# First recurrence steps with plain fp32 state products, weight conversions on VectorE, and four feed-forwards moved to later steps

## The chip, the cores and the metric

The kernel runs on one core of a Trainium2 chip. The metric is the time of one execution in microseconds, as the device reports it; lower is better. All times below are in microseconds unless they carry another unit. Engines are named as the profile names them: PE is TensorE (PEld its loading of the stationary operand), DVE is VectorE, ACT is ScalarE, POOL is GpSimd, and SP is the engine whose queue issues most transfers.

## The reference

The program is two layers. The first, where the change lies, is a GRU over 64 steps and a feed-forward with a ternary weight matrix, added to the input:

```python
def cell(h, x):
    gi = x @ W_ih + b_ih
    gh = h @ W_hh + b_hh
    i_r, i_z, i_n = jnp.split(gi, 3, axis=-1)
    h_r, h_z, h_n = jnp.split(gh, 3, axis=-1)
    r = jax.nn.sigmoid(i_r + h_r)
    z = jax.nn.sigmoid(i_z + h_z)
    n = jnp.tanh(i_n + r * h_n)
    h_new = (1.0 - z) * n + z * h
    return (h_new, h_new)
...
scale = jnp.mean(jnp.abs(weight))
w_t = jnp.clip(jnp.round(weight / (scale + EPS)), -1.0, 1.0)
w_ste = weight + jax.lax.stop_gradient(w_t * scale - weight)
return jnp.einsum('bsi,oi->bso', x, w_ste) + bias
...
x = x + ffn(gru(cond, x))
```

The batch is 128, the width 512, so a state is 128 x 512, and each gate is a product of a 128 x 512 operand with a 512 x 512 matrix. The second layer is a causal convolution over time, a router that sends each row to 6 of 64 experts, and a shared feed-forward; the change does not touch it.

## The kernel before

**The stages.** The GRU takes up to about 1255 us of the span, the convolution follows until about 1320, then the router, the shared feed-forward and the experts. All is one program; each engine runs its instructions in the order in which a scheduler has laid them out, and waits where an operand or a buffer is not ready.

**Products in three parts.** PE multiplies fp32 as such at one speed, and a rounded form (fp32r) faster. So the kernel splits each operand into a high part and a scaled low part and a mix of both, and forms a product as three fp32r products: high by high and low by low into one bank, mix by mix into a second, put together on DVE when the bank is read (`WHOLE`). A product of a 128 x 512 operand with a matrix is four matmuls, one for each 128 rows (`products`, L310 records each matmul). Step 0 alone uses plain fp32 products with the weights as they came from memory (`raw_i`, `raw_h`).

**Splitting a weight** (`convert`, L331): for each of the four pieces of 128 x 512, DVE masks off the low bits (`masked`, L321), ACT copies the result into the high plane, an engine subtracts it in place from the raw weight (L337: POOL for the three w_ih matrices, DVE for the three w_hh), ACT writes the scaled low plane (L338) and DVE the mix (L339). The cuts are a ring of four buffers (`stm`, later `cuts`). All 24 pieces are split ahead of the loop over steps: the w_ih matrices 0, 2, 1, then w_hh 0, 2 and 1. The input x of a step is split by `split_x` (masked on DVE, `xl` on POOL, `xs` on DVE), the turned state by `split_h` (DVE and ACT: `hcut`, `hh`, `hl`, `hs`).

**A step t** (L529): the state products for gates r, n and z (`state_gate`, c = 0, 2, 1), three groups of four matmuls each, are added to what the input products of this step have left in the banks; `split_x(t + 1)`; the cell on DVE and ACT (`cell_r`, `cell_n`, `cell_z`: h is overwritten); the feed-forward of the step before, two groups with the ternary matrix `sgn` (`ffn(t - 1)`); the input products of step t + 1 for gates n and r; the new h turned by four transposes (`turned_up`, L387) and split; the input products for gate z. That is 20 groups of four matmuls and four transposes. Eight banks of PSUM hold it all: two for each gate, one for the transposes (`pst`), one for the feed-forward (`psf`).

**Feed-forward.** `ffn` evacuates psf with the scale and the residual (L411, on DVE), and two stores on SP write the result, one to `x1c` for the convolution (L413), one to `out` (L417). The residual x of a step is loaded by `load_x` (L258) into one of seven slots, three in `io0` (`xn`) and four in a buffer `q` that held a raw w_hh and then the raw feed-forward weight; POOL adds the bias to it (`add_bias`, L263). `sgn` is made by `ternary` (L419) in step 1: four reductions, a product with ones, four comparisons and four `sgn` operations.

**Queues.** SP issues the loads of the weights and biases in the order of their use, then 32 stores of zeros (`x1c<-tab`, 16 KB), the feed-forward weight, and from then on the stores of each step and two transfers for the convolution (`toeplitz`). POOL issues the loads of x and of its transposed form (`xp`), between its own additions; its instructions run in their order, so a load that waits for a slot holds `xl`.

Of the kernel before, what the change touches and what calls it, by code (L numbers as in the profile page):

```python
# [45 lines left out]
def adaln_ffn_kernel(  # L46
# [32 lines left out]

    xts = dram.tile([T // 2, P, D], F32, name="xts")  # L80

    const = ctx.enter_context(tc.tile_pool(name="const", bufs=1))
# [123 lines left out]
    with (  # L206
# [18 lines left out]
        def planes(pool, name):  # L225
            return [pool.tile([P, KD, D], F32R, name=f"{name}{n}") for n in "hls"]
# [6 lines left out]
        st = stage.enter_context(tc.tile_pool(name="st", bufs=1))  # L233
        stm = stage.enter_context(tc.tile_pool(name="stm", bufs=4))
        raw_i = [st.tile([P, KD, D], F32, name=f"rawi{c}") for c in range(3)]
        late = ExitStack()
        raw_h = [
            st.tile([P, KD, D], F32, name="rawh0"),
            wi.tile([P, KD, D], F32, name="q"),
            late.enter_context(tc.tile_pool(name="late", bufs=1, side="right")).tile(  # L240
                [P, KD, D], F32, name="rawh2"
            ),
        ]
        zrow = stm.tile([P, D], F32, name="cut")

# [6 lines left out]

        more = []

        def load_x(t):
            r = (t - 1) % 7
            xn = io0.tile([P, D], F32, name="xn") if t < 3 or r > 3 else more[0][:, r]
            (nc.sync if t < 3 else nc.gpsimd).dma_start(out=xn, in_=x[:, t, :])  # L258
            xns[t] = xn

        def add_bias(t, after):
            with tc.issue_after(after.ins):
                nc.gpsimd.tensor_add(xns[t], xns[t], fb)  # L263

# [12 lines left out]
        load_halves(raw_i[2], w_ih[:, cols[2]])  # L277
        nc.sync.dma_start(out=h, in_=cond)
        load_halves(raw_i[1], w_ih[:, cols[1]])
        load_rows(raw_h[0], w_hh[:, cols[0]])  # L280
# [7 lines left out]
        repeated(bh[1], b_hh[cols[1]])  # L288
        load_xt(1, nc.sync)
        nc.gpsimd.memset(zrow, 0.0)  # L290
# [39 lines left out]

        def convert(raw, dst, engine, pool, name):  # L331

            for k in range(KD):
                cut = pool.tile([P, D], F32, name=name)
                masked(cut, raw[:, k])
                nc.scalar.copy(dst[0][:, k], cut)
                engine.tensor_sub(raw[:, k], raw[:, k], cut)  # L337
                nc.scalar.activation(dst[1][:, k], raw[:, k], AF.Copy, scale=SPLIT)  # L338
                nc.vector.scalar_tensor_tensor(  # L339
                    dst[2][:, k], cut, -1.0 / SPLIT, raw[:, k], ALU.mult, ALU.add  # L340
                )

        def split_x(t):

            xp = xps.pop(t)
            cut = xpp.tile([P, KD, B], F32, name="xcut", bufs=1)
            parts_of[t] = [xpp.tile([P, KD, B], F32R, name=f"x{n}", bufs=1) for n in "hls"]
            xh, xl, xs = parts_of[t]
            masked(cut, xp)
            nc.scalar.copy(xh, cut)  # L350
            return low_parts(nc.gpsimd, xl, xs, xp, cut)

        gis = {}

        def input_gate(t, c):

            xh, xl, xs = parts_of[t]
            wh, wl, ws = wih[c]
            a, b = banks(c)
            products(a, xh, wh, start=True)  # L360
            products(a, xl, wl, stop=c == 2)
            products(b, xs, ws, start=True, stop=c == 2)
            if c != 2:
                gis[t, c] = a, b
                return
            g = el0.tile([P, D], F32, name="gi")
            nc.vector.scalar_tensor_tensor(g, a, WHOLE, bin_, ALU.mult, ALU.add)
            nc.vector.tensor_add(g, b, g)
            gis[t, c] = g

        def state_gate(t, c, parts):

            hh, hl, hs = parts
            wh, wl, ws = whh[c]
            new = c == 2
            a, b = banks(c) if new else gis.pop((t, c))
            products(a, hh, wh, start=new)
            yield
            products(a, hl, wl, stop=True)
            products(b, hs, ws, start=new, stop=True)  # L380
            yield a, b
# [71 lines left out]
        def cell_n(t, ps, r):  # L453
            a, b = ps
            n = el0.tile([P, D], F32, name="n")
            if t == 0:
                nc.vector.tensor_add(n, b, bhn)
# [20 lines left out]

        load_x(0)

        x0 = xps.pop(0)
# [17 lines left out]
        r = cell_r(0, first[0])  # L499
        n = cell_n(0, first[2], r)  # L500
        cell_z(0, first[1], n)
        add_bias(0, split_x(1))
        for c in (0, 2, 1):
            convert(raw_i[c], wih[c], nc.gpsimd, stm, "cut")
        convert(raw_h[0], whh[0], nc.vector, stm, "cut")
        stage.close()
        load_xt(2)
        load_x(1)
        for c, name in ((2, "wh2"), (1, "wh1")):
            whh[c] = planes(  # L510
                wh0.enter_context(tc.tile_pool(name=name, bufs=1, reuse_waits="tile")), f"whh{c}"
            )
            with tc.tile_pool(name="cuts", bufs=4, reuse_waits="tile") as cuts:
                convert(raw_h[c], whh[c], nc.vector, cuts, "cut")
            if c == 2:
                late.close()
        sgn = wh0.enter_context(tc.tile_pool(name="sgn", bufs=1, reuse_waits="tile")).tile(
            [P, KD, D], F32R, name="sgn"
        )
        input_gate(1, 0)  # L520
        pieces = None
        input_gate(1, 2)
        turned = turned_up(h)
        pieces = split_h(turned)
        input_gate(1, 1)
        wf = wi.tile([P, KD, D], F32, name="q")
        load_rows(wf, wfT)

        for t in range(1, T):  # L529
            if t == 1:  # L530
                load_x(2)
            elif t + 3 < T:
                load_x(t + 3)
            if t + 2 < T:
# [3 lines left out]

            gates = [state_gate(t, c, pieces) for c in (0, 2, 1)]
            next(gates[0])  # L540
# [4 lines left out]
            if t + 1 < T:  # L545
                last_low = split_x(t + 1)
                add_bias(t, last_low)
            r = cell_r(t, ps_r)
            n = cell_n(t, ps_n, r)
            cell_z(t, ps_z, n)  # L550
            if t == 1:
                ternary(wf)
                more.append(wi.tile([P, KD, D], F32, name="q"))
                load_x(3)
                load_x(4)
            if t == T - 2:
                add_bias(T - 1, last_low)
            ffn(t - 1, pieces)
            if t + 1 < T:
                input_gate(t + 1, 2)  # L560
                input_gate(t + 1, 0)
                turned = turned_up(h)
                pieces = split_h(turned)
                input_gate(t + 1, 1)
            if t == T - TAIL:
# [1037 lines left out]
```

## Time and profile before

| what | value |
|---|---|
| median of three runs | 2502.7 (2502.47 to 2504.35) |
| the profiled execution | 2501.87 |
| its span, first to last instruction | 2500.2 |
| mean granted clock of TensorE | 0.994 |
| PE busy | 2455.9 (98%) |
| DVE busy | 1544.0 (62%) |
| ACT, POOL busy | 459.9, 457.6 (18% each) |
| bytes moved | 320.24 MB, 128 GB/s on average |

The profile is of one execution. A row of an order of time gives the start, the duration, the engine, the line in the kernel, the operation, its output and inputs by name with their shape, how many instructions were merged into the row, and in brackets how long the engine stood idle before it and what ended the wait. Matmuls overlap, so the distance between the starts of two groups is what a group costs, and the duration of the row is a little longer. A plain fp32 matmul shows as two records, an fp32r one as one. A row for a stretch of time gives for each engine the busy time in it, then the granted clock of TensorE, the share of the transfer engines that was busy, and GB/s.

### The profile page before, as it was taken

To read this page: it belongs to the slowest core of one execution; us is meant where nothing else is said; L and a number is where in the kernel's file an instruction comes from. 1 tells how busy PE (TensorE), PEld (TensorE's weight loads), DVE (VectorE), ACT (ScalarE), POOL (GpSimd) and SP (SyncE) were. 2 spreads that over 40 slices of the span, in tenths; PEclk is the share of its full clock that TensorE was granted. 3 is DMA by queue.
4 is the path that set the end of the run, shared out by engine and by line. 5 is a ranking of instruction groups with operands and counts; after the bars stand their busy time and mean duration, and the time that the engine had idled before them with its cause. 6 is when DMAs were issued, how large, how long until landed. Compare 5 with 4: busy or idle time off the path is not lost.

```text
span 2500.2 us, 32119 instructions
## 1 busy us (share of the span) xinstructions
PE 2455.9 (98%) x12333; PEld 1893.1 (76%) x12333; DVE 1544.0 (62%) x3058; ACT 459.9 (18%) x840; POOL 457.6 (18%) x476
## 2 busy tenths in 40 slices
PE   6899999999999999999989999999999999999999
PEld 3788888888888888888888668888776666666667
DVE  7777777767767777777667556666564333443344
ACT  5111111111111111111112322222221111111111
POOL 4221121121112112112221000000011222222220
PEclk8999999999999999999999999999999999999999
DMA  5433333333322222222388312222368999999962
GB/s 177 87 68 63 64 65 62 61 69 61 59 58 60 51 59 59 51 60 48 76 292 302 95 22 41 55 55 61 91 175 271 289 298 303 284 323 289 288 181 51
DMA packets 463754, 320.24 MB, mean 128 GB/s; under 512 B 316465, under 2 KB 384049, under 8 KB 461425
## 3 DMA queue, kind: packets, MB, share of 16 engines
q1 hardware_dynamic: 435264, 246.08, 34.4%
q0 software_dynamic: 28336, 72.11, 12.8%
q8 instruction: 97, 1.59, 0.3%
q14 instruction: 57, 0.46, 0.1%
HBM read 232.39 MB, written 90.98 MB: 129 GB/s over the span
## 4 chain that ended last, share of the span: by engine, by line
PE 94%; DVE 1%; DMA 1%; issue 0%; SPq 0%; ACT 0%; POOL 0%; DVEq 0%; ACTq 0%
PE psa L310 9%; PE psx L310 9%; PE psw L310 9%; PE psw L762 7%; PE psx L762 7%; PE psz L762 7%; PE psf L310 5%; PE psy L310 5%; PE psz L310 5%; PE psb L310 4%; PE y L762 4%; PE py L1488 3%; PE pg L1462 3%; PE pu L1462 3%; PE y L939 2%; PE psc L188 2%
## 5 line engine op out<-in xcount | busy, mean ns | idle before, releaser
L328 DVE SCALAR_TENSOR_TENSOR xs<-xl,xcut 128x512 fp32r<-128x512 f32 x63 | 109.9, 1744 | 84.7 <-POOL xl L327 84.7
L1472 DVE SCALAR_TENSOR_TENSOR a<-a,rw,pu 128x352 f32<-128x352 f32 x32 | 18.6, 581 | 213.0 <-PE pu L1462 213.0
L321 DVE TENSOR_SCALAR hcut<-pst 128x512 int32<-128x512 int32 x64 | 44.3, 692 | 147.2 <-PE pst L387 147.2
L395 ACT CAST hh<-hcut 128x512 fp32r<-128x512 f32 x64 | 39.8, 621 | 401.6 <-DVE hcut L321 390.6
L1044 POOL DMA_DIRECT2D out_dram<-hid x32 | 27.8, 1026 | 450.6 <-issue 333.7
L327 POOL TENSOR_TENSOR xl<-xp,xcut 128x512 fp32r<-128x512 f32 x63 | 87.2, 1384 | 123.4 <-PE psa L310 99.4
L450 ACT ACTIVATE rz<-rz 128x512 f32<-128x512 f32 x64 | 40.5, 633 | 351.1 <-DVE rz L449 349.3
L258 POOL DMA_DIRECT2D q<-in_x_dram x34 | 18.3, 538 | 450.0 <-DVE hcut L321 157.8
L1488 PE MATMUL py<-wd,aeT 128*64 128x512 f32 (+1 forms) x384 | 88.8, 597 | 0.0
L258 POOL DMA_DIRECT2D xn<-in_x_dram x27 | 14.5, 538 | 386.5 <-DMA out_dram<-xn 200.6
L1462 PE MATMUL pg<-wg,xeT 128*64 128x352 f32 x512 | 81.2, 459 | 0.0
L1462 PE MATMUL pu<-wu,xeT 128*64 128x352 f32 x512 | 81.2, 459 | 0.0
L1499 POOL DMA_INDIRECT out_dram<-ys,idxp x32 | 45.9, 1435 | 182.7 <-DMA out_dram<-ys,idxo 75.1
L1499 POOL DMA_INDIRECT out_dram<-ys,idxo x32 | 45.4, 1419 | 175.9 <-DMA out_dram<-ys,idxp 150.5
L310 PE MATMUL psf<-sgn,hh 128*128 128x512 f32 x256 | 71.3, 398 | 5.4 <-DVE sgn L438 5.2
L310 PE MATMUL psa<-wih1h,xh 128*128 128x512 f32 x252 | 73.7, 414 | 0.0
L310 PE MATMUL psx<-whh0h,hh 128*128 128x512 f32 x252 | 70.1, 400 | 3.5 <-ACT hh L395 3.5
L310 PE MATMUL psx<-wih0h,xh 128*128 128x512 f32 x252 | 68.2, 393 | 4.6 <-ACT xh L350 4.6
L1462 PEld LDWEIGHTS pg<-wg,xeT 128*64 128x64 f32 x512 | 36.4, 136 | 47.3 <-issue 46.4
L310 PE MATMUL psf<-sgn,hl 128*128 128x512 f32 x256 | 71.0, 400 | 0.0
L802 ACT ACTIVATE g<-psx 128x256 f32<-128x256 f32 x80 | 30.7, 384 | 217.5 <-DVE aT L809 156.1
L463 ACT ACTIVATE n<-n 128x512 f32<-128x512 f32 x64 | 40.5, 633 | 162.9 <-DVE n L462 162.9
(389 smaller groups left out, 6180.0 us busy)
## 6 DMA issues: line engine op xcount, KB each, us to landing
wg<-in_w_gate_dram SPq DMA_DIRECT2D x64, 704.0 KB
wu<-in_w_up_dram SPq DMA_DIRECT2D x64, 704.0 KB
wd<-in_w_down_dram SPq DMA_DIRECT2D x64, 512.0 KB
xc<-x1c SPq DMA_DIRECT2D x32, 512.0 KB
xp<-in_xT_dram POOLq DMA_DIRECT2D x62, 256.0 KB, 2.9
tab<-hid SPq DMA_DIRECT2D x56, 256.0 KB
wd<-in_w_down_dram SPq DMA_DIRECT2D x64, 192.0 KB
q<-in_x_dram POOLq DMA_DIRECT2D x34, 256.0 KB, 4.5
```

What stands on the lines that cost most here:

```text
L188: i = nc.tensor.matmul(ps[rows, j].rearrange("p h (u t) -> p h u t", u=2), xcs[sl % NCB][:, rows, g * 4 + j], tzs[sl % NCB][:, :, :, g * 4 ...
L310: i = nc.tensor.matmul(ps, lhs[:, k, :], rhs[:, k, :], start=start and k == 0, stop=stop and k == KD - 1, skip_group_check=True,)
L321: return nc.vector.tensor_scalar(dst.bitcast(I32), src.bitcast(I32), LOW, None, ALU.bitwise_and)
L327: i = engine.tensor_sub(lo, full, cut)
L328: nc.vector.scalar_tensor_tensor(mix, lo.bitcast(F32), -SPLIT, cut, ALU.mult, ALU.add)
L450: nc.scalar.activation(r, r, AF.Sigmoid)
L463: nc.scalar.activation(n, n, AF.Tanh)
L762: i = nc.tensor.matmul(ps.rearrange("p (j b) -> p j b", b=P) if len(r.shape) == 3 else ps, lhs(k), r, start=(first and k == 0), stop=(k == ...
L939: nc.tensor.matmul(gu.rearrange("p (j b) -> p j b", b=P), swr[:, k].rearrange("p w n -> p (w n)"), rows[:, k], start=(k == 0), stop=(k == ...
L1462: nc.tensor.matmul(acc[halves[j]], self.xeT[:, k, halves[j]], self.ws[j][which][:, k, :], start=(k == 0), stop=(k == KD - 1),)
L1488: nc.tensor.matmul(py[halves[j]], self.aeT[:n, c, halves[j]], self.ws[j][2][:n, c, :], start=(c == 0), stop=(c == len(ech) - 1),)
L1499: nc.gpsimd.indirect_dma_start(out=out, out_offset=bass.IndirectOffsetOnAxis(ap=(idxp[:CAP] if j == 0 else idxo)[:, q : q + 1], axis=0), i ...
```

## The change

Five things are changed, all in the GRU.

- In step 1 the state products of all three gates, in step 2 that of gate z, are plain: one fp32 product of the turned state `hT` with the raw weight (`PLAIN`). w_hh 0 is converted ahead of the loop, after the inputs and the turning for step 1 have been recorded; w_hh 2 at the end of step 1; w_hh 1 at the end of step 2.
- `convert` subtracts on DVE for all six matrices, into a buffer of its own (`lo`), so that the raw weight stays whole; the rings of cuts have two buffers instead of four. `split_x` uses DVE for the inputs of steps 1 to 3 and POOL from step 4 on.
- `ternary` is run in step 4 (`LATE`) instead of step 1; the feed-forward weight is loaded at the end of step 2.
- The feed-forwards of steps 0 to 3 move to steps 5 to 8, each behind the one that belongs there. For this the turned state of steps 0 to 3 is stored to memory (`htd`, on SP) and loaded again (on POOL), then split by `late_ffn`.
- The loads of x for the first feed-forwards, three on SP, are gone from the start; `load_for` loads what a step needs from step 4 on, all on POOL. The transposed x of step 1 is loaded ahead of the last of the w_ih matrices.

The scheduler lays out the new instructions on each engine; from step 9 on every engine has the same instructions in the same order as before. The core of the diff:

```diff
-        stm = stage.enter_context(tc.tile_pool(name="stm", bufs=4))
+        stm = stage.enter_context(tc.tile_pool(name="stm", bufs=2))
...
-        more = []
+        PLAIN = {1: (0, 2, 1), 2: (1,)}
+        LATE = 4
+        more, hts = [], {}
+        placed = [2]
+        def slot():
+            r = placed[0] % 7
+            placed[0] += 1
+            return io0.tile([P, D], F32, name="xn") if r > 3 else more[0][:, r]
         def load_x(t):
-            r = (t - 1) % 7
-            xn = io0.tile([P, D], F32, name="xn") if t < 3 or r > 3 else more[0][:, r]
-            (nc.sync if t < 3 else nc.gpsimd).dma_start(out=xn, in_=x[:, t, :])
-            xns[t] = xn
+            xns[t] = slot()
+            nc.gpsimd.dma_start(out=xns[t], in_=x[:, t, :])
+        def load_for(step):
+            load_x(step - 1)
+            if step - 1 < 2 * LATE:
+                load_x(step - 1 - LATE)
+                hts[step - 1 - LATE] = slot()
+                nc.gpsimd.dma_start(out=hts[step - 1 - LATE], in_=htd[step - 1 - LATE])
...
+        load_xt(1, nc.sync)
         load_halves(raw_i[1], w_ih[:, cols[1]])
...
-                engine.tensor_sub(raw[:, k], raw[:, k], cut)
-                nc.scalar.activation(dst[1][:, k], raw[:, k], AF.Copy, scale=SPLIT)
+                lo = pool.tile([P, D], F32, name="lo")
+                nc.vector.tensor_sub(lo, raw[:, k], cut)
+                nc.scalar.activation(dst[1][:, k], lo, AF.Copy, scale=SPLIT)
...
-            return low_parts(nc.gpsimd, xl, xs, xp, cut)
+            return low_parts(nc.vector if t < LATE else nc.gpsimd, xl, xs, xp, cut)
...
+            if c in PLAIN.get(t, ()):
+                products(b, hT, raw_h[c], start=new, stop=True)
+                yield
+                yield None if new else a, b
+                return
...
+        def next_inputs(t):
+            if t > 0:
+                input_gate(t + 1, 2)
+                input_gate(t + 1, 0)
+            else:
+                input_gate(1, 0)
+                input_gate(1, 2)
+            turned = turned_up(h)
+            hT = pieces = None
+            if t < LATE:
+                hT = io0.tile([P, KD, B], F32, name="xn")
+                nc.scalar.copy(hT, turned)
+                nc.sync.dma_start(out=htd[t], in_=hT.rearrange("p k b -> p (k b)"))
+            if t > 0:
+                pieces = split_h(turned)
+            input_gate(t + 1, 1)
+            return pieces, hT
+        def late_ffn(t):
+            hh, hl = (el0.tile([P, KD, B], F32R, name=f"h{n}") for n in "hl")
+            cut = el0.tile([P, KD, B], F32, name="hcut")
+            full = hts.pop(t).rearrange("p (k b) -> p k b", k=KD)
+            masked(cut, full)
+            nc.scalar.copy(hh, cut)
+            nc.vector.tensor_sub(hl, full, cut)
+            ffn(t, (hh, hl))
...
-            if t == 1:
+            if t == LATE:
                 ternary(wf)
                 more.append(wi.tile([P, KD, D], F32, name="q"))
-                load_x(3)
-                load_x(4)
-            ffn(t - 1, pieces)
+                for n in range(1, 3):
+                    load_for(t + n)
+                add_bias(t + 1)
+            if t > LATE:
+                ffn(t - 1, pieces)
+                if t - 1 < 2 * LATE:
+                    late_ffn(t - 1 - LATE)
...
+            if t in (1, 2):
+                c = 3 - t
+                whh[c] = planes(
+                    wh0.enter_context(tc.tile_pool(name=f"wh{c}", bufs=1, reuse_waits="tile")),
+                    f"whh{c}",
+                )
+                with tc.tile_pool(name="cuts", bufs=2, reuse_waits="tile") as cuts:
+                    convert(raw_h[c], whh[c], cuts)
```

## The prediction

> **What bounds the kernel now.** I read the busy shares, then who waited for whom on PE in the first 200 us, then the order of time on PE, DVE and POOL around the places that the change touches.
>
> ```profile
> PE 2455.9 (98%) x12333; PEld 1893.1 (76%) x12333; DVE 1544.0 (62%) x3058; ACT 459.9 (18%) x840; POOL 457.6 (18%) x476
> ```
>
> PE is busy for 98% of the span, so time can only be won by less PE work or where PE stands still. The second view, the stretches of ten microseconds (columns: PE, PEld, DVE, ACT, POOL, granted clock, DMA share, GB/s), shows where that is; the third names the waits.
>
> ```profile
> 20.00:30.00 10.00, 4.11 (x9) 1.58 (x8) 7.13 (x11) 5.68 (x9) 6.76 (x5) 0.76 0.95 340
> 50.00:60.00 10.00, 6.47 (x24) 4.93 (x23) 10.00 (x19) 6.66 (x13) 0.00 (x0) 0.83 0.01 2
> 80.00:90.00 10.00, 5.99 (x12) 3.90 (x13) 7.21 (x11) 0.62 (x1) 3.32 (x6) 0.66 0.29 88
> 100.00:110.00 10.00, 10.00 (x48) 8.21 (x47) 6.17 (x9) 1.15 (x2) 3.08 (x3) 1.00 0.55 98
> ```
>
> ```profile
> PE psz L310 <- DVE gi L488: 5.9, 1, 5.9
> PE psf L310 <- DVE sgn L438: 5.2, 4, 3.1
> PE psx L310 <- ACT xh L350: 4.6, 1, 4.6
> PE psx L310 <- ACT hh L395: 3.5, 1, 3.5
> PE psx L310 <- DVE hl L327: 1.7, 1, 1.7
> ```
>
> Up to 90 us PE is busy for 63.4 us only, part of that at a clock of 0.66 to 0.83; from 100 us on it is full. All waits end on DVE or on ACT behind DVE, which has the weights to split, one state to compute and the ternary matrix to make. So the start is the only stretch that matters. I measure it between marks on PE: the first state product of each step.
>
> ```profile
> 28.85 5.29 PE L310 MATMUL psz<-rawh,hcut 128*128 128x512 f32 x8 [5.89 <-DVE gi L488]
> 33.98 3.60 PE L310 MATMUL psb<-q,hcut 128*128 128x512 f32 x8
> ...
> 56.44 2.08 PE L310 MATMUL psx<-whh0h,hh 128*128 128x512 f32 x4 [3.53 <-ACT hh L395]
> ...
> 88.40 1.88 PE L310 MATMUL psx<-whh0h,hh 128*128 128x512 f32 x4
> ...
> 108.11 1.08 PE L310 MATMUL psx<-whh0h,hh 128*128 128x512 f32 x4
> ```
>
> Step 1 starts at 56.44, step 2 at 88.40, step 3 at 108.11; from there a step takes 18.87 and step 9 starts at 221.35. A group of four split matmuls takes 0.91 to 0.93 from start to start. A plain group (eight records, 0.43 apart, 3.44) replaces the three split groups of a gate (2.79), so a plain gate costs 0.65 more.
>
> **The price of a conversion on VectorE**, from the order of time on DVE:
>
> ```profile
> 55.66 0.75 DVE L321 TENSOR_SCALAR cut<-q 128x512 int32<-128x512 int32 x2
> 56.32 1.28 DVE L337 TENSOR_TENSOR q<-q,cut 128x512 f32<-128x512 f32 x2
> 57.53 1.28 DVE L339 SCALAR_TENSOR_TENSOR whh1s<-cut,q 128x512 fp32r<-128x512 f32 x2
> 58.73 0.75 DVE L321 TENSOR_SCALAR cut<-q 128x512 int32<-128x512 int32 x2
> ```
>
> Two pieces in 3.07: mask 0.33, subtraction 0.605, mix 0.60, start to start. ACT's two copies for a piece take 0.57 each, less than DVE's 1.54.
>
> **The change, part by part. 1: up to step 1's state product.** Splitting whh2 and whh1 (8 pieces) leaves this stretch; the subtractions of the 12 wih pieces come from POOL (1.26 to 1.3 each) to DVE. In the new order of instructions DVE has, from its first mask (5.12, when the first half of the weight has landed) to the end of step 0's state: 17 masks, 16 subtractions, 16 mixes and 11 operations of the cell and the gates at 0.60: 5.6 + 9.7 + 9.6 + 6.6 = 31.5, so 36.6. Waits, walked along the queues: 0.4 for the second x, moved ahead of the last third of w_ih (2.75 MB have to be in by then; the rates sum to 2.8 MB at 10 us and DVE asks at 11.8), 0.4 for PE's psy, 0.5 at the hand-overs to ACT: 37.9. Two POOL additions of biases stand in the stretch and may each block a DVE operation (below): 1.2; a ring of two cuts instead of four makes DVE wait for ACT around the table load: 1.0. That is 40.1, then 0.5 for transposes and 0.7 for the copy of the turned state: step 1 starts at 41.3. Bounds: 37.8 without any of these extras; 43.8 if DVE is idle for as large a share as now (37.1 busy of 44.2 up to the same point: 31.5 / 0.84).
>
> **2: PE from there to step 9.** A step without feed-forward is 17.01 (18.87 less two groups, 1.86). Steps 1 to 8 together still hold eight feed-forwards: 8 x 18.87 = 151.0. Plain gates: three in step 1, one in step 2, 4 x 0.65 = 2.6. So 153.6: unhindered, step 9 starts at 194.9 instead of 221.35.
>
> **3: hand-overs in steps 1 to 3.** DVE now splits whh2 in step 1 and whh1 in steps 2 and 3, 6.2 each, beside 17 us of PE work. For the state of step 1 PE asks 15.8 after the step's start (three plain groups, 10.3, and six split ones, 5.5); DVE begins on r at 3.8 and has eleven operations of the cell (6.6), a mask of x (0.3) and the rest of whh2 (4.3), which is 15.0, and 0.2 of waits: 0.6 early. The same count gives 0.1 for hh of step 2, behind ACT's copies of whh1 and of the turned state, and 0.4 for the state of step 2. The ternary load can start when the last plain product has read the buffer that it reuses (67.3); it stands on SP behind the second store of the turned state, whose data are there at 56. Now it was issued at 61.95 and its 1 MB had passed by 66.3; 4.4 later is 71.9, DVE asks at 72.5. Margins this thin: 0.5 lost, between 0 and 6 (each of three missed by 2).
>
> **4: the clock.** PE stands nearly idle for 3.4 ahead of step 1. A gap of 1.94 left the next eight records at 0.46 each; gaps of 3.53 and 5.89 were followed by 2.08 for four split ones instead of 1.08, and by 5.29 instead of 3.60. Bounds 0 and 1.8; I take half, 0.9. The Trainium skill (TensorE: Matmul & The Clock Gate, "What's actually happening") says that an idle window of about 3.4 us halves the clock, and that transposes do not count as activity; by it the sum would have the full 1.8. The trace agrees for gaps of 3.5 and over.
>
> **5: steps 5 to 8 with two feed-forwards.** PE's work is moved, not added, but each late one brings a mask (0.42), a subtraction and an evacuation (0.7 each) on DVE, a copy on ACT, two loads and a 1.29 addition on POOL, two stores on SP. There is one psf bank: the late products start five split matmuls (1.15) after the first, whose result DVE must have taken by then. Now:
>
> ```profile
> 126.50 0.54 POOL L258 DMA_DIRECT2D xn<-in_x_dram  x1 [15.90 <-DMA out_dram<-xn]
> 127.05 1.30 POOL L327 TENSOR_TENSOR xl<-xp,xcut 128x512 fp32r<-128x512 f32 x1
> 128.30 1.30 POOL L263 TENSOR_TENSOR q<-q,fb 128x512 f32<-128x512 f32 x1
> ...
> 128.39 1.76 DVE L328 SCALAR_TENSOR_TENSOR xs<-xl,xcut 128x512 fp32r<-128x512 f32 x1 [1.82 <-POOL xl L327]
> ...
> 137.41 0.75 DVE L411 SCALAR_TENSOR_TENSOR q<-psf,scale,q 128x512 f32<-128x512 f32 x1 [0.44 <-PE psf L310]
> ```
>
> POOL's load waits until a store has left its slot, 5.8 to 7.2 after the evacuation; xl is queued behind that load, xs behind xl, and the whole cell behind xs. Here, with the load 0.5 before the step's start at 127.0, DVE is still 0.44 early at psf. With two pairs of stores on SP (the out issue holds it for 2.8) the second lands 9 to 10.3 after the first evacuation, so the load comes between 0.5 before the next step's start and 0.8 after: 0 to 0.7 lost a step in steps 6 to 8. The second addition on POOL may hold xs for another 1.25, of which 0.44 is free: up to 0.8 in steps 6 and 7. In step 5 the four comparisons and four sgn (0.51 and 0.75) stand ahead of the cell, and it is about 1.4 late. Sum 1.4 + 1.2 + 1.2 + 0.4 = 4.2; bounds 0 and 12 (three a step, if landings slip as the queue doubles). By the Trainium skill (SBUF — State Buffer, "Who interferes with whom") a VectorE instruction with two SBUF inputs and a GpSimd one that reads SBUF lock each other out whole, whichever comes first. The 1.76 of xs, against 0.68 alone, agrees; by this rule the second addition costs its full 1.25 a step if POOL wins each time, and nothing if xs slips in between.
>
> **6: the rest.** After step 9 every queue holds the same instructions in the same order, so the shift is kept to the end: the chain that ended last is 94% PE. The plain gates of step 0 remain. The four stores of the turned state (256 KB) pass while the queue carries only 16 KB fills: nothing, by the DMA share of 0.00 to 0.01 there; if that cover failed, the ternary load would be late, priced in part 3.
>
> **Sum.** 41.3 + 153.6 + 0.5 + 0.9 + 4.2 = 200.5 against 221.35: 20.8 less. The profiled run took 2501.9 (span 2500.2), 0.8 under the median, so 2481.1 for it, **2482** for the median.
>
> **Rivals.**
> - All of part 5 is hidden and the clock holds: 5 less, 2477, down to 2474 with the early bound of part 1. For it: DVE is idle 5 of 19 in a step. Against it: the single psf bank, with 0.44 to spare.
> - VectorE stays the bound through steps 1 to 3: step 1 at 43.8 and the margins of part 3 missed by 2 each: 8 worse, 2490. For it: DVE is at 10.00 of 10 in 50 to 60 now; against it: 14 us of conversions fewer ahead of step 1.
> - Slower: the second pair of stores in steps 5 to 8 holds POOL's load, xl and the cell. Without part 5 the gain is 25.0, so it must cost 6.2 in each of four steps; the store would have to land 16 after the first evacuation, where one pair needs at most 7.2. At 7.5 a step it gives 2508. POOL's wait is already the last one before xs, which speaks for it; that a pair now lands 5.8 to 7.2 after the evacuation, and two need not land one behind the other, against it.
>
> **The numbers.** Forecast 0.45 (2478 to 2487), hidden 0.22, VectorE-bound 0.25, slower 0.06, no change 0.02 (0.2%, 5 us, is about what a measurement of this kernel can tell). Range 2474.5 to 2493.5: down by all of parts 3 to 5 and half of the way to part 1's lower bound (0.5 + 0.9 + 4.2 + 1.8), up by the upper bounds of parts 3 and 4 and half of the way in parts 1 and 5 (5.5 + 0.9 + 1.2 + 3.9).
>
> **What would show it.** Right: the first plain product of step 1 near 41, step 2 near 61, step 5 near 113, step 9 near 200, sgn gone from PE's waits. Wrong: PE waiting for hh or transposes in steps 1 to 3 (part 3), or for psf's evacuation in steps 5 to 8 by more than 2 a step (part 5).

## The result and the profile after

The changed kernel takes 2492.26 us (2489.2 to 2494.03) against 2502.47 (2501.88 to 2504.35) before: a ratio of 0.9956, with a 95% interval of 0.9942 to 0.997. That is 10.2 us faster, about half of the 20.8 that the sum gave. The profiled execution took 2492.93 with a span of 2491.2 and a mean granted clock of 0.996, so it stands 0.7 above the median.

The page's busy shares of the changed kernel, and its waits on PE in the first 260 us (engine, tile and line that waited, what it waited for; total, times, longest):

```profile
PE 2456.5 (99%) x12317; PEld 1889.8 (76%) x12317; DVE 1548.1 (62%) x3077; ACT 462.8 (19%) x847; POOL 443.0 (18%) x468
```

```profile
PE psf L328 <- ACT rz L499: 9.8, 4, 3.3
PE pst L411 <- DVE h L501: 2.2, 1, 2.2
```

PE is busy for as long as before to within 0.6 us (2456.5 against 2455.9), in a span that is 9.0 shorter. The waits of 3.5 to 5.9 us at the start, on hh, xh and gi, are gone. A new kind stands at the head of the list: four waits at `psf`, 9.8 us together, that the kernel before did not have. The order of time on PE shows where they are:

```profile
42.24 5.40 PE L328 MATMUL psy<-rawh,xn 128*128 128x512 f32 x8 [0.67 <-ACT xn L537]
47.48 3.60 PE L328 MATMUL psz<-rawh,xn 128*128 128x512 f32 x8
63.45 1.49 PE L328 MATMUL psx<-whh0h,hh 128*128 128x512 f32 x4
...
115.13 1.08 PE L328 MATMUL psx<-whh0h,hh 128*128 128x512 f32 x4
...
129.94 1.16 PE L328 MATMUL psf<-sgn,hh 128*128 128x512 f32 x4 [3.28 <-ACT rz L499]
131.24 2.07 PE L328 MATMUL psf<-sgn,hl 128*128 128x512 f32 x4
141.19 1.08 PE L328 MATMUL psx<-whh0h,hh 128*128 128x512 f32 x4
...
154.96 1.88 PE L328 MATMUL psf<-sgn,hh 128*128 128x512 f32 x4 [2.26 <-ACT rz L499]
...
179.68 1.17 PE L328 MATMUL psf<-sgn,hh 128*128 128x512 f32 x4 [2.17 <-ACT rz L499]
...
202.90 2.02 PE L328 MATMUL psf<-sgn,hh 128*128 128x512 f32 x4 [2.04 <-ACT rz L499]
...
213.96 1.08 PE L328 MATMUL psx<-whh0h,hh 128*128 128x512 f32 x4
```

Step 1 starts at 42.24 (56.44 before), step 5 at 115.13, step 9 at 213.96 (221.35 before). The four late products are the second feed-forwards of steps 5 to 8, and PE stands still ahead of each. The windows of these four steps (length, busy time of PE, PEld, DVE, ACT, POOL, granted clock, DMA share, GB/s) say what a step cost:

```profile
115.13:141.19 26.06, 22.78 (x94) 17.93 (x93) 20.77 (x28) 3.55 (x6) 10.89 (x12) 0.93 0.49 104
141.19:165.99 24.80, 22.54 (x94) 18.02 (x93) 16.39 (x23) 3.55 (x6) 5.89 (x7) 0.93 0.49 101
165.99:189.35 23.36, 21.19 (x94) 16.80 (x93) 16.39 (x23) 3.55 (x6) 5.88 (x7) 1.00 0.48 84
189.35:213.96 24.61, 22.57 (x94) 18.08 (x92) 14.81 (x22) 3.55 (x6) 4.64 (x6) 0.93 0.51 108
```

Such a step holds 18.87 and two more groups, 1.86: 20.73 of PE work. So 98.83 - 4 x 20.73 = 15.9 us are lost here: 9.75 as the four waits, the other 6.2 nearly all in the three steps with a granted clock of 0.93, which lose about 1.9 each beyond their wait (26.06 - 20.73 - 3.28 = 2.05; 1.81; 1.84), against 0.46 in the step with 1.00.

The account of the gain: in the profile before, step 3 starts at 108.11, and two steps more put step 5 at 145.85. The changed kernel is there at 115.13, 30.7 earlier, with four feed-forwards (4 x 1.86 = 7.4) still to be done: a gain of 23.3. Steps 5 to 8 give 15.9 of it back, and 7.4 are left at step 9.

What holds PE there is seen in step 6, in the order of time of SP, POOL, DVE and PE together:

```profile
129.06 0.73 DVE L435 SCALAR_TENSOR_TENSOR q<-psf,scale,q 128x512 f32<-128x512 f32 x1
...
133.43 0.75 DVE L435 SCALAR_TENSOR_TENSOR q<-psf,scale,q 128x512 f32<-128x512 f32 x1 [1.64 <-PE psf L328]
...
134.63 4.37 SPq L441 DMA_DIRECT2D out_dram<-q  x1
...
142.43 0.54 POOL L275 DMA_DIRECT2D q<-htd  x1 [2.61 <-DMA out_dram<-q]
142.99 1.31 POOL L345 TENSOR_TENSOR xl<-xp,xcut 128x512 fp32r<-128x512 f32 x1
144.24 2.53 POOL L281 TENSOR_TENSOR q<-q,fb 128x512 f32<-128x512 f32 x2
...
144.33 3.00 DVE L346 SCALAR_TENSOR_TENSOR xs<-xl,xcut 128x512 fp32r<-128x512 f32 x1 [3.04 <-POOL xl L345]
147.76 0.69 DVE L472 SCALAR_TENSOR_TENSOR rz<-psx,br 128x512 f32<-128x512 f32 x1
...
154.07 0.74 DVE L435 SCALAR_TENSOR_TENSOR xn<-psf,scale,xn 128x512 f32<-128x512 f32 x1
```

POOL's load of the turned state (142.43) waits for the second store of the step before. It comes 1.24 after the start of step 6 at 141.19. `xl` stands behind that load, `xs` behind `xl`, the whole cell behind `xs`, and the evacuation of `psf` behind most of the cell. It ends at 154.81, and 0.15 later PE starts the late product that needs the bank. The waits name ACT's rz L499 as the releaser because that event is the last before; the instruction that clears the bank is DVE's at L435.

### The profile page after: what moved, and what is told of

Same layout as the page of the kernel before. It is cut to its first block, busy times and chain, and to the rows that moved or that the text cites. A ratio compares the mean times of both kernels' runs of the same rounds, so it can differ in the third digit from the quotient of the medians.

```text
span 2491.2 us, 32129 instructions
## 1 busy us (share of the span) xinstructions
PE 2456.5 (99%) x12317; PEld 1889.8 (76%) x12317; DVE 1548.1 (62%) x3077; ACT 462.8 (19%) x847; POOL 443.0 (18%) x468
## 4 chain that ended last, share of the span: by engine, by line
PE 95%; DMA 2%; DVE 2%; issue 1%; POOL 0%; ACT 0%; SPq 0%; DVEq 0%; POOLq 0%; ACTq 0%
PE psa L328 9%; PE psx L328 9%; PE psw L328 9%; PE psw L813 8%; PE psz L813 8%; PE psx L813 8%; PE psb L328 5%; PE psy L328 5%; PE psf L328 5%; PE psz L328 5%; PE y L813 4%; PE py L1539 3%; PE pg L1513 3%; PE pu L1513 3%; PE y L990 2%; PE psc L190 2%
## 5 line engine op out<-in xcount | busy, mean ns | idle before, releaser
L853 ACT ACTIVATE g<-psx 128x256 f32<-128x256 f32 x80 | 30.7, 383 | 217.5 <-DVE aT L860 158.5
L328 PE MATMUL psw<-wih2l,xl 128*128 128x512 f32 x252 | 70.8, 397 | 0.0
L328 PE MATMUL psy<-wih0s,xs 128*128 128x512 f32 x252 | 68.1, 392 | 1.5 <-DVE rz L470 1.5
```

Of the source, the lines that this page charges most:

```text
L328: i = nc.tensor.matmul(ps, lhs[:, k, :], rhs[:, k, :], start=start and k == 0, stop=stop and k == KD - 1, skip_group_check=True,)
```

## The experiments

Two theories stood against each other for the loss in steps 5 to 8. Q: the queue is late, that is, POOL's loads hold `xl` and the cell, so whatever comes at the end of the cell is late too. B: the bank is tight, that is, the late product asks for the single `psf` only five matmuls (1.15 us) after the first, and more distance would hide a late cell. The other experiments test the start and the clock. Diffs are against the changed kernel. A time without a range is that of one execution, beside a kernel before of 2502.3 to 2503.4.

The starts of the steps on PE, us, from the profiled execution of each kernel. It took 2492.93 for the changed kernel, 2475.66 for e3_both and 2474.93 for e9_best. From the start of step 9 to the end of the span, where all but e4_nolate, which stores its constants there, run the same instructions, the ten kernels took 2276.5 to 2280.5; so the starts tell small differences better than the whole time of one execution does.

| kernel | step 1 | step 5 | step 6 | step 7 | step 8 | step 9 | whole |
|---|---|---|---|---|---|---|---|
| changed kernel | 42.24 | 115.13 | 141.19 | 165.99 | 189.35 | 213.96 | 2492.26 |
| e1_apart | 42.09 | 116.27 | 137.00 | 158.53 | 179.25 | 199.96 | 2480.58 |
| e2_xlfirst | 42.20 | 116.18 | 143.06 | 163.86 | 184.66 | 205.46 | 2485.85 |
| e3_both | 40.89 | 114.32 | 135.06 | 155.77 | 176.48 | 197.19 | 2477.23 |
| e4_nolate | 41.79 | 115.59 | 134.49 | 153.36 | 172.23 | 191.11 | 2472.17 |
| e5_onebias | 42.17 | 115.97 | 140.51 | 162.70 | 185.00 | 208.47 | 2487.3 |
| e6_poolsub | 50.63 | 123.78 | 149.66 | 173.30 | 200.16 | 221.53 | 2499.74 |
| e7_warm | 42.22 | 113.37 | 137.83 | 164.65 | 188.53 | 211.88 | 2494.06 |
| e8_whh0late | 39.14 | 111.62 | 137.52 | 160.76 | 185.59 | 208.16 | 2487.51 |
| e9_best | 39.17 | 113.28 | 134.03 | 154.74 | 175.46 | 196.17 | 2475.32 |

### The second feed-forward behind the input products

```diff
+            if LATE < t <= 2 * LATE:
+                late_ffn(t - 1 - LATE)
             turned = turned_up(h)
...
                 ffn(t - 1, pieces)
-                if t - 1 < 2 * LATE:
-                    late_ffn(t - 1 - LATE)
```

> Changed: in steps 5 to 8 the late feed-forward's products stand behind the six input groups of gates n and r (5.4 us) instead of five matmuls (1.15 us) behind the first feed-forward. Steps 5 to 8 took 26.1, 24.8, 23.4 and 24.6 us in the changed kernel, where their PE work is 20.7. Theory Q (the queue: POOL's x low part waits behind loads that wait for the late stores, and DVE's cell behind it, so the whole cell is late and the reuse of psf is only where it shows): step 5 falls to about 21, but the late evacuation now comes 3 to 4 us later, its stores land later, POOL's load with them, and from step 6 on the wait moves to the transposes for h: steps 6 to 8 still 22 to 24.5 each, step 9 begins near 205. Rival B (the bank: one psf bank used again too soon): the waits are gone, all four steps 20.7 to 21, step 9 begins near 198.

Steps 5 to 8 took 20.73, 21.53, 20.72 and 20.71, and the kernel 2480.58. The only wait of PE between 100 and 230 us, and step 6 on DVE, POOL and PE:

```profile
PE psw L328 <- DVE n L483: 0.5, 1, 0.5
```

```profile
137.00 1.08 PE L328 MATMUL psx<-whh0h,hh 128*128 128x512 f32 x4
...
140.59 0.54 POOL L267 DMA_DIRECT2D q<-in_x_dram  x1 [7.36 <-DMA out_dram<-q]
141.15 1.30 POOL L345 TENSOR_TENSOR xl<-xp,xcut 128x512 fp32r<-128x512 f32 x1
...
145.76 0.68 DVE L472 SCALAR_TENSOR_TENSOR rz<-psx,br 128x512 f32<-128x512 f32 x1
...
153.48 1.09 PE L328 MATMUL psf<-sgn,hh 128*128 128x512 f32 x4
```

What Q expected of this kernel, 22 to 24.5 for each of steps 6 to 8, did not come. The edit moves the load of the turned state behind `xl` as well, but a load of x still stands ahead of it and is even later than in the changed kernel: 3.6 after the step's start. DVE takes `psx` 8.8 into the step, 2.2 later than in step 6 of the changed kernel; PE waits 0.5, and the step is 0.8 longer than its work. The late product now stands six groups of input products, 5.4 us, behind the first (in step 5 it starts at 131.95, the first of the six at 126.50); with 5.4 us of distance in place of 1.15 a later cell costs 0.8 in one step and nothing in the others. So B holds.

### POOL's loads behind xl

```diff
-            elif t == 2 * LATE:
-                for n in range(1, 4):
-                    load_for(t + n)
-            elif LATE + 1 < t < 2 * LATE:
-                load_for(t + 1)
...
                 last_low = split_x(t + 1)
+                if LATE + 1 < t <= 2 * LATE:
+                    with tc.issue_after(last_low.ins):
+                        for n in range(1, 4 if t == 2 * LATE else 2):
+                            load_for(t + n)
```

> Changed: POOL's order alone. In steps 6 to 8 the loads for the next step stand behind the x low part instead of ahead of it. Theory Q: POOL's x low part starts 0.7 before the next step as in the kernel before, DVE reads psx 3 us into the step instead of 6.5, PE's wait ahead of the late products falls from 2.0 to 2.3 to at most 1 in steps 6 to 8, the half clock behind it goes too; steps 6 to 8 take 20.8 to 22 instead of 23.4 to 24.8, step 5 stays at 26. Step 9 begins near 207 instead of 214. Rival B (the bank): no more than 0.5 us a step, step 9 near 213.

Steps 6, 7 and 8 took 20.80 each; step 5, which the edit does not touch, took 26.88. Step 6 again:

```profile
142.39 1.40 POOL L345 TENSOR_TENSOR xl<-xp,xcut 128x512 fp32r<-128x512 f32 x1 [13.34 <-PE psa L328]
143.74 1.10 POOL L267 DMA_DIRECT2D q<-in_x_dram  x2
...
144.00 0.68 DVE L346 SCALAR_TENSOR_TENSOR xs<-xl,xcut 128x512 fp32r<-128x512 f32 x1
...
146.04 0.69 DVE L472 SCALAR_TENSOR_TENSOR rz<-psx,br 128x512 f32<-128x512 f32 x1 [0.84 <-PE psx L328]
...
153.48 0.75 DVE L435 SCALAR_TENSOR_TENSOR xn<-psf,scale,xn 128x512 f32<-128x512 f32 x1 [0.45 <-PE psf L328]
```

`xl` now starts 0.7 ahead of the step at 143.06, `xs` takes 0.68 because the additions come later, and DVE waits for PE at gates r and n and at `psf`, not the other way round. So Q names a real cause too: in steps 6 to 8 the loss needs both, the late queue and the tight bank, and taking away either one removes it. In step 5 the distance to the bank alone removes it (20.73 in the first experiment).

### Both edits

The two diffs above together.

> Both edits: late products behind the input groups, and POOL's loads behind the x low part. Theory Q: neither the queue nor the bank holds the cell; steps 5 to 8 take 20.7 to 21.5 each, step 9 begins at 199 to 201, some 14 us earlier than in the changed kernel; the time is 2476 to 2481. Rival (the late work itself loads DVE or the transfers too much, wherever it stands): step 9 begins at 206 or later, 2485 or more.

2477.23 (2475.66 to 2477.77), a ratio of 0.9899 (0.9882 to 0.9916) to the kernel before. PE waits for nothing between 100 and 230 us. Two of its windows, of steps 5 and 6:

```profile
114.32:135.06 20.74, 20.74 (x94) 16.87 (x93) 20.12 (x27) 3.55 (x6) 9.78 (x10) 1.00 0.35 81
135.06:155.77 20.71, 20.71 (x94) 16.95 (x92) 17.73 (x24) 3.56 (x6) 6.08 (x8) 1.00 0.56 113
```

PE is busy for the whole of each step at a clock of 1.00: the 20.73 of PE work that the prediction put into a doubled step is confirmed, and the second feed-forwards cost nothing beyond it.

### Steps 5 to 8 without the second feed-forward

This kernel leaves out the feed-forwards of steps 0 to 3, with the stores and loads of the turned state, the late loads of x and the late additions, and stores a constant into their rows; the ternary matrix is still made in step 4.

```diff
-                for t in (step - 1, step - 1 - LATE) if step - 1 < 2 * LATE else (step - 1,):
+                for t in (step - 1,):
                     nc.gpsimd.tensor_add(xns[t], xns[t], fb)
...
-                if t - 1 < 2 * LATE:
-                    late_ffn(t - 1 - LATE)
```

> The late feed-forwards are left out: no store and load of the turned state, no late x, no late addition, none of their 32 matmuls; the rows of steps 0 to 3 are stored with a constant in steps 10 to 13. PE work of steps 5 to 8 is then 18.87 each. Theory Q: steps 6 to 8 take 18.9, step 5 at most 20.5 (the ternary matrix is made there): step 9 begins at 191 to 193, 21 to 23 us earlier than in the changed kernel, of which 7.4 is work left out and the rest, 14 to 15, what the doubling costs. Rival (what holds steps 5 to 8 is the ternary matrix and the new order of loads, not the doubling): steps 6 to 8 still 2 us longer than 18.87 each.

Steps of 18.90, 18.87, 18.87 and 18.88, without a wait. Step 9 starts 22.85 earlier than in the changed kernel; 7.4 of that is work left out, so 15.4 is what the doubling cost beyond its work: the 15.9 of the windows less the 0.5 by which step 5 starts later here. The comparisons of the ternary matrix in steps 4 and 5 cost nothing by themselves.

### One addition less on POOL

The late row gets no bias, which is left out.

```diff
-                for t in (step - 1, step - 1 - LATE) if step - 1 < 2 * LATE else (step - 1,):
+                for t in (step - 1,):
                     nc.gpsimd.tensor_add(xns[t], xns[t], fb)
```

> The changed kernel without the second addition of a step on POOL: the late x of steps 0 to 3 gets no bias (that is left out of the result). Queue and psf order stay. In the changed kernel x's mixed part took 3.00 us on DVE in steps 6 and 7, behind both additions. If the lock between POOL's additions and DVE is what doubled: mix back to 1.76, DVE reads psx 1.2 earlier in steps 6 and 7, step 5 loses less too (its DVE rows stretched to 1.5 to 1.8 come down); the waits ahead of the late products fall from 3.3, 2.3, 2.2, 2.0 to about 1.5, 1.0, 1.0, 2.0 and steps 5 to 8 take 3 to 6 us less together. If the queue of loads alone is it: the mix starts no earlier, the four steps change by less than 1 us together.

The four steps took 24.54, 22.19, 22.30 and 23.47, 92.5 in all, 6.3 less. Step 6 on DVE, and the waits on PE from 0 to 230 us:

```profile
143.67 1.77 DVE L346 SCALAR_TENSOR_TENSOR xs<-xl,xcut 128x512 fp32r<-128x512 f32 x1 [3.06 <-POOL xl L345]
```

```profile
PE psf L328 <- ACT rz L499: 6.4, 4, 2.3
```

`xs` goes from 3.00 to 1.77: one addition less holds it 1.23 less, which is its full 1.25. So in the changed kernel both additions went ahead of `xs`. The waits of PE fell from 9.75 to 6.4, so 3.4 of the 6.3 is waiting; the rest is the clock, which fell in one step here and in three there. How often it falls is not settled by the second addition alone: the next three kernels, which have both additions in these steps, lost 14.8, 15.6 and 13.6 in them, with two, one and two falls. Against these and the 15.9 of the changed kernel, the 9.6 lost here is 4.0 to 6.3 less, and that is as close as the runs give the second addition's share; the rest stays with the late load and with step 5.

### The subtractions of w_ih back on POOL

```diff
-                nc.vector.tensor_sub(lo, raw[:, k], cut)
+                engine.tensor_sub(lo, raw[:, k], cut)
...
-            convert(raw_i[c], wih[c], stm)
+            convert(raw_i[c], wih[c], stm, nc.gpsimd)
```

> The changed kernel with the subtractions of the three input matrices back on POOL; all else stays, the scheduler lays the rest out anew. By the count of DVE's work (what sets the start of step 1): DVE loses 12 x 0.605 = 7.3 us, but its mixes, with two inputs in SBUF, run beside POOL's subtractions, where they took 1.74 instead of 0.64 in the kernel before; with half of them caught that is 6.6 back, and ACT's low planes wait for POOL's 1.27 a piece: step 1 starts at 41 to 44, no clear gain or loss. Rival (moving the conversions to DVE is what brings step 1 forward): step 1 starts at 47 or later. Rival (DVE is the bound and any relief helps): at 37 or earlier.

Step 1 starts at 50.63, and the kernel takes 2499.74. PE's longest wait, and two of DVE's rows:

```profile
PE psy L328 <- DVE rz L470: 7.5, 1, 7.5
```

```profile
26.72 3.41 DVE L358 SCALAR_TENSOR_TENSOR wih1s<-cut,lo 128x512 fp32r<-128x512 f32 x2 [1.16 <-POOL lo L356]
32.57 3.43 DVE L358 SCALAR_TENSOR_TENSOR wih1s<-cut,lo 128x512 fp32r<-128x512 f32 x2 [0.57 <-POOL lo L356]
```

A pair of mixes takes 3.41 where it took 1.28, and DVE waits for POOL's results besides, 5.2 in all. Not all of the 3.41 is the subtractions' doing: POOL's two additions of biases (27.87 for 1.71 and 33.73 for 1.72), which the changed kernel has too, lie beside the second mix of each pair. The expectation, 41 to 44, missed, and the picture that DVE is relieved by POOL's subtractions falls: in the changed kernel DVE does these 12 itself and reaches step 1 8.4 us earlier. All of the gain that is left at step 9 goes with this edit (221.53, against 221.35 before). With the plain products, but without the subtractions on DVE, nothing is won by step 9. The rings have two buffers here, and POOL waited for ACT's low planes (1.62 and 1.20); what its subtractions would cost with the four buffers of the kernel before was not run.

### Work for PE ahead of step 1

Eight small products of ones into the idle `psf`, between the last input group and the transposes.

```diff
+        def keep_busy(count, after):
+            ps = ps_f.tile([P, D], F32, name="psf")
+            with tc.issue_after(after.ins):
+                for _ in range(count):
+                    nc.tensor.matmul(ps[:, :P], ones, ones, start=True, stop=True)
...
-            input_gate(t + 1, 1)
+            i = input_gate(t + 1, 1)
+            if t == 0:
+                keep_busy(8, i)
```

> Eight small products of ones, into the idle psf bank, between the last input product of step 1 and the transposes, where PE waited 2.2 us. If the low clock of the first plain product (5.4 us in the changed kernel, 6.5 in two runs of variants, 3.6 at full clock) comes of the gap ahead of it: it takes 3.6 to 4.2, and step 5 begins about 2 us earlier after step 1's start (71 instead of 72.9). If it does not come of the gap: unchanged. Step 1's start is unchanged at about 42.

```profile
38.52 1.95 PE L530 MATMUL psf<-ones 128*128 128x128 f32 x16
42.22 3.70 PE L328 MATMUL psy<-rawh,xn 128*128 128x512 f32 x8 [0.67 <-ACT xn L544]
```

Step 1 starts where it did, but its first gate takes 3.70, not 5.40, and step 5 starts 71.15 after it, not 72.89: 1.74 saved, which was the clock's price. Steps 5 to 8 lost 15.6 again, and step 9 starts 2.1 earlier. The whole time, 2494.06, does not show it (the changed kernel took 2489.2 to 2494.03), because this one execution took 3.3 longer from step 9 to the end, 2280.5 against 2277.2.

### w_hh 0 converted behind the state of step 0

```diff
-        cell_z(0, first[1], n)
+        done = cell_z(0, first[1], n)
...
-        convert(raw_h[0], whh[0], stm)
+        with tc.issue_after(done.ins):
+            convert(raw_h[0], whh[0], stm)
```

> The four pieces of w_hh 0 are converted on DVE behind the state of step 0 instead of ahead of it; in the changed kernel three of them and a mask, 5 us, stood ahead. Everything else stays. By the count of DVE's work: the state of step 0 comes 4 us earlier, step 1 starts near 38, PE has step 2's first input products to fill its gap, DVE still delivers the state of step 1 in time: step 5 begins 4 to 6 us earlier, at 109 to 111, and so does everything behind. Rival (DVE is the bound through steps 1 to 3, so work moved behind only moves the wait): PE waits for the state or hh in steps 1 to 3 by as much, step 5 begins at 114 or later.

```profile
39.14 3.70 PE L328 MATMUL psy<-rawh,xn 128*128 128x512 f32 x8 [0.21 <-ACT xn L537]
...
77.17 1.19 PE L328 MATMUL psx<-whh0h,hh 128*128 128x512 f32 x4 [2.75 <-ACT hh L419]
```

Step 1 comes 3.1 earlier and at full clock: the new order of instructions puts six products of step 2's input, 36.50 to 37.87, ahead of the transposes and two behind them, so that hardly a gap is left. Then 2.75 is given back as a wait for `hh` ahead of step 3: the 5 us of conversion moved behind the state of step 0 use up the thin margin there. What is left at step 5 is 3.5, a little less than the 4 to 6 expected, and 2487.51 in the whole.

### All three together

The diffs of the two feed-forward edits and of w_hh 0.

> Late products behind the input groups, POOL's loads behind the x low part, and w_hh 0 converted behind the state of step 0: the edits of the first, second and eighth run together. By the marks of the runs: step 5 begins near 111.6 and each of steps 5 to 8 takes 20.7, so step 9 begins at 194 to 196, 2 to 5 us earlier than with the first two edits; the time is 2472 to 2476. If the edits overlap (the wait for hh ahead of step 3 grows, or the later start of steps 5 to 8 was slack): 2476 to 2479.

2475.32 (2474.2 to 2476.39), a ratio of 0.9889 (0.9872 to 0.9905): faster than both kernels. Steps 5 to 8 take 20.75, 20.71, 20.72 and 20.71. The same wait ahead of step 3, but this time with a clock that follows it down:

```profile
77.22 2.02 PE L328 MATMUL psx<-whh0h,hh 128*128 128x512 f32 x4 [2.75 <-ACT hh L419]
```

Step 3 takes 18.75, where it took 17.18 without that (94.35 - 77.17). Step 9 starts 1.0 earlier than with the two feed-forward edits alone, not the 2 to 5 expected, and the interval overlaps theirs, so whether w_hh 0 late is worth anything on top of them is not settled.

## Why the prediction was right and wrong

The direction held and the time lies in the range, but the sum was 11.8 off for the profiled execution (2481.1 against 2492.93), and one term of it is the reason: part 1 was 0.9 too low, parts 2 to 4 0.8, part 5 11.7, and the rest of the kernel came 1.6 shorter. That the median still lies in the range is in part luck, since part 5 went 3.9 beyond its own upper bound of 12; the slowest of the five executions, 2494.03, is outside. By the prediction's own sign of being wrong, more than 2 of wait at `psf` in steps 5 to 8, its part 5 was wrong in all four (3.28, 2.26, 2.17, 2.04).

- Part 1, the start: 42.24 against 41.3, within its bounds. DVE's queue sets it: with the conversion of w_hh 0 out of the stretch it is 39.14. The count is good only for a queue that POOL does not hold up: with 12 subtractions taken off DVE it is 50.63.
- Parts 2 and 3, PE's work and the thin margins: 42.24 to 115.13 is 72.89 against 70.7 + 0.5 + 0.9 = 72.1. PE waited for nothing in steps 1 to 4. The margins held; that they were thin shows in the wait for `hh` ahead of step 3 once more conversion was put there.
- Part 4, the clock: half of 1.8 was taken, and 1.8 was lost (5.40 against 3.60 for the first gate). The fillers show the cause: with only transposes in the 3.5 us ahead of the gate (38.72 to 42.24) the clock fell, with 1.95 us of products there it did not. The bound itself was too low. In the first two feed-forward experiments, where PE works the same up to there, the same gate took 6.62 and 6.50, up to 3.0 more than 3.60; this is why their step 5 starts 1.1 later. The rule of the Trainium skill that transposes do not count as activity stands in another section than the prediction names (TensorE: Matmul & The Clock Gate, "Part 4: PE-mode transpose"); it gave the better number, but no run here tells transposes from an empty gap, so the rule by itself is not shown.
- Part 5, the doubled steps: **the term that failed**. 4.2 was put in, with 12 as the upper bound; 15.9 was lost. The mechanism was the one described, and four of its sizes were off.

  First, the second addition was taken at 0.8, its 1.25 less the 0.44 that DVE was early; both additions went ahead of `xs` each time in steps 6 and 7 (3.00), and the 0.44 had already been set against the late load (a shift of up to 1.3 was priced at up to 0.7), so it was counted twice. One addition less gave up to 6.3 back. By the rule of the Trainium skill (SBUF — State Buffer, "Who interferes with whom"), whoever comes first holds the other off for the whole instruction; of the two outcomes that the prediction drew from it, the dearer one came. The 3.00 agrees with a hold for whole instructions, but not plainly with the order: `xs` stood from 144.33, and the second addition, which started at 145.49, still went ahead of it.

  Second, the second store was put at 9 to 10.3 after the first evacuation; POOL went on 12.6 after it (142.43 against 129.79), because the second evacuation is itself 4.4 behind the first, and POOL goes on 8.2 after that, one pair of stores having taken 5.8 to 7.2. So the load came 1.24, 1.17 and 2.27 after the start of steps 6, 7 and 8, not between 0.5 ahead and 0.8 behind. With these sizes the prediction's own chain nearly closes: the load's shift from 0.5 ahead, plus the second addition in steps 6 and 7, less 0.44, makes 2.5, 2.5 and 2.3, and PE waited 2.26, 2.17 and 2.04.

  Third, in step 5 only the ternary matrix was counted against the cell, 1.4 late; it lost 5.3. POOL's additions there lie beside DVE's rows and stretch them:

```profile
115.72 3.17 POOL L281 TENSOR_TENSOR xn<-xn,fb 128x512 f32<-128x512 f32 x2
...
115.97 1.78 DVE L346 SCALAR_TENSOR_TENSOR hs<-hl,hcut 128x512 fp32r<-128x512 f32 x1
117.66 1.77 DVE L462 SCALAR_TENSOR_TENSOR sgn<-q,half,n 128x512 fp32r<-128x512 f32 x1
...
124.79 3.19 POOL L281 TENSOR_TENSOR q<-q,fb 128x512 f32<-128x512 f32 x2 [0.72 <-DMA q<-in_x_dram]
...
125.19 1.67 DVE L486 TENSOR_TENSOR n<-n,gi 128x512 f32<-128x512 f32 x1
```

  Three rows of the changed kernel's step 5 that take 0.69 to 0.75 elsewhere take 1.67 to 1.78 here, 3.1 together. In the kernel without the second feed-forward two of the three are as long (1.78 and 1.66); DVE empties `psf` 12.5 into the step there, 1.5 earlier than here, and nothing asks for the bank, so nothing is lost.

  Fourth, the sum had no clock in part 5 at all: about 1.9 in each of three steps.
- Part 6, the rest: step 9 to the end took 1.6 less than before (2277.24 against 2278.85), with the same instructions; that is inside the 2276.5 to 2280.5 of the ten kernels, and nothing can be read from it.
- The rivals: VectorE as the bound of steps 1 to 3 did not come (no wait there). The hidden case, 2477, is the time of the kernel with both feed-forward edits, though there the clock did not hold (5.95 for the first gate). The slower rival had the right mechanism, too: the second store pair. It needed 6.2 in each of four steps, counted from a gain of 25.0; the four lost 4.0 each.

What was missed when reading the profile before is the line that part 5 quoted: DVE's evacuation was 0.44 early with one addition and one pair of stores. Each of the things that the change added to this chain, 1.23 by the second addition, 1.7 by the later load (from 0.5 ahead of the step's start to 1.24 behind it) and 3.1 by the stretched rows of step 5, is larger than that by itself.

## What to carry to other kernels

Work that is moved onto a single buffer is not priced by its duration but by the distance to the buffer's last user: count the groups between the two uses and ask which queued instruction clears it. On an in-order queue a load that waits for a store belongs behind the small operations that others wait for; here the distance removed all but 0.8 us of the loss in four steps, and the order the loss of three. A short wait of a full TensorE is to be priced with the clock behind it: of the four waits here three, 2.0 to 3.3 us long, cost 1.8 to 2.1 more each.

## What the hardware showed that was not expected

- **When a wait lowers the clock.** The waits at `psf` in the changed kernel and in the experiments, from 1.96 to 3.57 us long, are seventeen. After ten of them a row of four matmuls took 1.55 to 2.07 where 1.08 to 1.10 is usual; after seven it took 1.16 to 1.20. The length does not decide: 1.96 is among the ten, 3.29 among the seven; behind the four shorter waits, 0.22 to 1.42, no row was slow. The Trainium skill (TensorE: Matmul & The Clock Gate, "What's actually happening") says that the activity window runs freely, so that it matters where in it the work falls; the mix agrees with that. It also puts the low clock behind at least one idle window of about 3.4 us, and there the runs differ: a gap of 1.96 was enough. What does decide it, no run here shows.
- **Two additions in a row on POOL.** Behind one addition `xs` took 1.77, behind two 3.00, alone 0.68. Where DVE got in between the two, the POOL pair took 3.17 to 3.19, not 2.53. Either way one engine waits for the whole of the other's instruction.
- **The price of POOL's help.** A subtraction took 1.26 to 1.3 on POOL and 0.6 on DVE; 12 of them on POOL made step 1 start 8.4 us later, and the rows show DVE both waiting for their results (5.2 in all) and held in its mixes (3.41 for a pair in place of 1.28, a part of it beside additions of biases).
